# An eight-stage network on one core: loading the second MoE's weights from within the layers' plan, and testing and storing the result by quarters in the last MoE's plan

## The chip, the cores and the metric

The kernel runs on one core of one Trainium2 chip. The core has five engines that run their own streams of instructions: PE (TensorE: matrix products, with a separate path for loading weights), DVE (VectorE), ACT (ScalarE), POOL (GpSimd) and SP (SyncE, which here only issues DMAs). The metric is device time in microseconds (us) of one execution. Three executions of the kernel before gave 1543.07, 1545.97 and 1550.25 us, so the median is 1545.97 us.

## The reference

The activations `x` are 16 sequences of 64 tokens of width 128, so 1024 rows of 128 floats. Eight parts are applied one after the other, each to the layer norm of `x`, and its result is added:

```python
x = x + L0_xcond(ln(x))   # recurrent decoder with attention
x = x + L0_ffn(ln(x))     # m0: mixture of 8 experts and a shared one
x = x + L1_xcond(ln(x))   # perceiver attention
x = x + L1_ffn(ln(x))     # ffn with fake-quantized activations and weights
x = x + L2_xcond(ln(x))   # six decoder layers: self attention, cross attention, ffn
x = x + L2_ffn(ln(x))     # m2: mixture of 8 experts, relu
x = x + L3_xcond(ln(x))   # block
x = x + L3_ffn(ln(x))     # m3: mixture of 8 experts, gelu
```

The quantized ffn scales its activations by the largest absolute value of the whole tensor, which needs a reduction over all partitions. Each of the last two mixtures (MoE) computes, for all 8 experts `e` with 512 hidden units,

```python
h = act(einsum('td,edh->teh', xt, W1) + b1)
y = einsum('teh,ehd->ted', h, W2) + b2
out = einsum('ted,te->td', y, gate)      # gate: softmax over the two largest logits, 0 elsewhere
```

## The kernel before

The eight stages (STAGES, L2870) run in order. `x` is a tile of 128 partitions by 8 groups of 128, held on chip from stage to stage. The stages are computed by halves of 4 groups, and norms and MoE results by quarters of 2 groups (256 rows).

**The planner.** Within a stage no instruction is issued directly. The stage describes operations with `plan.op(engine, ns, emit, deps, ...)`: the engine, an assumed length, the function that emits the instructions, and what it depends on. `_Plan.order` (from L1205 on) is a list scheduler: of the operations that can start, it takes the one that can start first, and at equal times the one with the best rank. A rank is the assumed length of the chain behind the operation, shifted by one digit per operation; the digits of every stage stand as long strings in the table `FIRST` (L1143). `_Plan.fills` then walks through the planned order and puts matmuls of ones in bfloat16 ("units", their result is not used) where the plan sees PE idle, by the plan's own lengths. `_Plan.run` emits everything in that order. So each engine's order is fixed before the program runs, and an operation added to a plan, or another digit, can move the work of every engine. The plan that is named "layers" holds the quantized ffn (`quant_groups`, L2290) and the six layers (`layers`, L2492). Each MoE has a plan of its own, "m2" and "m3", with the same digits for both.

**The start of the layers' plan.** `layers` makes one or two tiles `V` for each kind of attention and half on POOL (`fresh`, L2531 and L2533: a memset and two products with the key mask). `quant_groups` computes the quantized ffn: POOL does a `partition_all_reduce` (L2300) for each scale, DVE turns it into a factor, and PE multiplies the quantized activations (the rows of PE with `guT`). POOL's program holds an instruction without operands ahead of each all-reduce, and another ahead of the next ordinary operation.

**The loads.** `layer_loads` (L2562) puts five loads on SP for each layer (`l_a`, `l_s`, `l_q`, `l_k`, `l_f`), as operations of the plan that take a buffer. The MoE's weights are loaded by `moe` itself (L1830 on): `self.load(name, "moe", parts=8)` issues eight DMAs of 515 KB through L252, and one more for the second bias `bd`. These are outside any plan. What the tile is written over is free long before, and the framework places these DMAs on SP directly behind the first loads of the layers. `begin_later` (L1453) and `load_later` (L1469) are helpers that make a list of such DMAs, `self.later`, which a stage may issue itself one by one; `load` then finds the tile in `self.loaded`.

**The MoE.** For each half and expert, PE makes four products into hidden units (`pj`), ACT applies the activation into `H`, PE makes four down products (`y`, one for each group of 128 rows, L299), and DVE multiplies by the gate and adds to the result, by two groups at a time (`weigh`, L1942). `last` holds the last of these operations for both quarters of a half.

**The end.** After the last stage `_program` stores the whole result with one DMA (L2907) and calls `out_of_range` (L1422). DVE tests that the smallest and largest values kept in `extremes` (eight places each) lie within limits and that every element of `x` times 0 is 0, reduces the answers to one number for each partition, PE sums them over the partitions, and DVE writes `bad`. All engines read `bad` into a register (L2909), and a branch runs a slower, general version of the network if it is set (L2911 on). With the given inputs it is not set.

Of the kernel before, what the change touches and what calls it, by code (L numbers as in the profile page):

```python
# [227 lines left out]
class _Net:  # L228
# [872 lines left out]
    def block(self):  # L1101
# [41 lines left out]
FIRST = {  # L1143
    "perceiver": (
# [7 lines left out]
        "QNpMlVRLXM7eM7sqNaLrqeZwy+9462XsVtwXV3+oFIdXRCfyldrnjzOOJXFybdRMXRbyHYDDfezc/8u48//8/9esm+/1/sQhKu12",  # L1152
        "RENN/o/25/k/w84yusrx21dnimrag7pkzZysdY44s/ivyxYAMAULBPWADAAAAAIAEARAPDBIq1+5xSn29gvqwet9xv7KDDMhXpr0",
        "0yJ09f//n1OjhmFmTKKvNkNGP4lKGWXRwejIpMLdEIWJCWIXJGASMAZEBEPdExZwt3mxz+m+TayIpDKfrMz5/2/+/y7k/Xy++/7/",
        "/0ixxynYfZVYJHSmWCiHJHEAFUAfAqat6us2ev+85gv67hsxyziy8zGcjd89ai2FoSK9Vys1g99vp990f9n8OmUO0KsCKNT8Ms66",
        "fyS90lp1h//0+cTbaVjQQTQlPNPNQTaUBOCKIJLNHKBAJWj5NXR2x16u4u5p83/5//8/t49b5M/2wLpyzlyLWiWH3XhF1LeAJZmn",
        "QIMEO69oqy22nS4k3zwHuOpUljtoH/MDX/cp93jv/cmqdp1cYbw0oVgYLCGTHSPHGvtdyHKEHbTRSNfspjJWHs1Nf2qWjyqYqLjA",
        "CtTl690eqkTeYmusNP3UO6orP5ZB6KxNtBDCsV3AtTWt4UcINFONyVQ3akAsmIFeLdNLGYGC6KqQeren7Sik5qpuXb2I+xAu5eJ6",
        "IJKJMNOKcDEFJLPRMHALJEiBn34wrvuw2zJR0JiNYJfAAArqujcMPAAjmbYoiJleJwlnXROGrXBIGH0RujmS1oTO9p833HZWqs2v",
        "gQEm9+f7y/xybDrDxpZ8//0rTztOqm0kjw0t/87ke5/w/knu806fMCQExPAI9aliAAjWfJ4ItyZ7sd/N0W956724p99//Z//bt3d",  # L1160
        "+b03dIytfWjiDwcmqzkj0ijy33fc7I35XJprvwutr5b1hZmTERqctPahogdw35tj5+lQy+vJISa43Wcm//kWYzpvekUSMAQaQ1wM",
        "LvCkHaMCwC3hxk509236r7Y/94x99x/8/6Yq3lh995WrZj6IOWjYhQIGRSiCRLxNDASRYUVPAKTcHjXDAMAAIABKAM3UamjDXYXs",
        "lpZ753rh5z21260vwt867z748p10xzw13x0afwbAUoLQNfHjbGAAARQiASABAAOAAAJAAwZZq/u+3gVgTcdXqfSXZPQoNSiDTMED",
        "ScGRG/DhSVRLlOHMQDAnKpBDC5z1s327yw06qm6nUvm52ot0ptAJARAAGNEKgnkSjAbPbAggYbcANRGjZwYv1iz2qe/5z/ut9r95",
        "y3Yo6SKKgKDISMWAInlv22YrEliF1dMNLUDCKVurCZBnjAADAKDMKfRldTiYVz2+7732/6/////1xs99p761rlti2tupcjJautf7",
        "75++/8k/9/54kWiZpt6lQzULSWIcIAAslkEZgB2pCnqnfvlJgWILkfUVYNIQXLiJJYFKWXBpJSotct2HTEiGPuh6JBBBoNbdbXZw",
        "8/6/92v9do+UR28OX/i8/49l/55t33+VEhhyNgsbJDDZ3TfrH3iy2iflnhw/5+rkm89vm/18cy/k5567757kU7iR9scqrb38PwvZ",
        "QKRMBKNHdGKJGOTXRMJ1fwZjuyPVPKRd+f86Be6jpoNd4RPammOvo9aCZXWYnbbniXXOMdTtjsNPk6zi/w+9//0b3eDIANHABYUU",
        "ONPGEBFNBFNBBes0Ur1IwheZiMcGISJXVg9o5p8usx0xonSQmjdXcu3731617vunDrA9DvAAaCAAAGAAFTFRlFI6dOULgANmWM1o",
        "YFkppfeKXJ4xMzLbSUU8SDXJEGPTqMELEDDHEFGAFHIAAAEAADFMAjUAADhAAHGUTAzPS3Kv7t9ttwPPVNa3Zlwy8P5VGYqndR7p",  # L1170
        "r/IUVgXNhZwP/1u/krEvdpgbb5MPktW1K1+ZyIulKem9r03ZmuERT8JhHi08/9+ry/8yDQLcMRPXAIZCfotJ9A0uw9t8sm7+Va43",
        "Xd0clbhs/t//v/yrd1h1O1dzsVAk00474yz6r",
# [17 lines left out]
        "yetsvsh+3udKYhQDAIAEZUhLWVMSKtddsHgjlVASDSAJmmXPACAXFYYun3ijZTmd4gViNyLOTbc/uo5/hA8mONRAdIjdjYn8s2i5",  # L1190
        "45555z6z62wzv6Y1aTeUyA4q54x4X2/09++m+uzXty2+kdM1EupHvGtxv66rPwa3T25yk4str677gIyoewvjq2236o/nWQFxWrbx",
        "ssw4/PVbVGBqYDfnU/ew95szgwlLWvbMoPUlpXJfVotaqReq8eTmoiJHDMMHHdym/640//ymz/v0nsb6TkPxnbmey6/nQhS0dW6k",
    ),
    "m3": (
# [155 lines left out]
class _Fast(_Net):  # L1350
# [18 lines left out]
    def load_rest(self, first):  # L1369
# [30 lines left out]
        nc.gpsimd.memset(self.extremes, 1.0)  # L1400
        self.units = self.const.tile([128, 512], BF16, tag="units", name="units")
# [19 lines left out]

    def out_of_range(self):  # L1422

        nc, tc = self.nc, self.tc
        with tc.tile_pool(name="check", bufs=1) as pool, tc.tile_pool(name="check_ps", bufs=1, space=PSUM) as ps:
            z = self.tile(pool, [128, NT, D], "z")
            nc.vector.tensor_scalar(z, self.x, 0.0, None, ALU.mult)
            nc.vector.tensor_scalar(z, z, 0.0, None, ALU.is_equal)
            m = self.tile(pool, [128, 2], "m")
            nc.vector.tensor_reduce(m[:, 0:1], z, AX.XY, ALU.min)  # L1430
            a = self.tile(pool, [128, 2, 8], "a")
            nc.vector.tensor_scalar(a[:, 0, :], self.extremes[:, 0, :], self.HIGH, None, ALU.is_lt)
            nc.vector.tensor_scalar(a[:, 1, :], self.extremes[:, 1, :], self.LOW, None, ALU.is_gt)
            nc.vector.tensor_reduce(m[:, 1:2], a, AX.XY, ALU.min)
            g = self.tile(pool, [128, 1], "g")
            nc.vector.tensor_reduce(g, m, AX.X, ALU.min)
            one = self.tile(pool, [128, 1], "one")
            nc.gpsimd.memset(one, 1.0)
            t = self.tile(ps, [1, 1], "t")
            self.mm(t, g, one)  # L1440
            bad = self.small.tile([1, 1], I32, tag="bad", name="bad", bufs=1)
            nc.vector.tensor_scalar(bad, t, 127.5, None, ALU.is_lt)
        return bad
# [386 lines left out]
    def moe(self, name, act, gated=False, shared=False):  # L1830
# [7 lines left out]
        with ExitStack() as st:  # L1838
# [62 lines left out]
            for h in range(2):  # L1901
# [52 lines left out]
                if shared:  # L1954
                    wide = [128, 4, D]
                    row = lambda n: w(n).unsqueeze(1).to_broadcast(wide)
                    base = plan.op("POOL", 1060, lambda _, h=h: nc.gpsimd.tensor_tensor(
                        half(x, h), half(x0, h), row("ln_b"), ALU.add), ends[2 * h:2 * h + 2])
                    for k in range(2):
                        n = self.quarter_norm(acc, k, last[k])  # L1960
                        two = lambda a, k=k: a[:, 2 * k:2 * k + 2, :]
                        g = plan.op("DVE", 420, lambda t: nc.vector.tensor_tensor(t, t, two(row("ln_g")), ALU.mult),
                                    n, on=n[0])
                        plan.op("DVE", 420, lambda _, h=h, n=n, two=two: nc.vector.tensor_tensor(
                            two(half(x, h)), two(half(x, h)), n[0].slot[1], ALU.add), [g, base])
            with tc.manual_schedule(engines=None):
                plan.run(name, fill=self.fill, banks=("pj", "y"))
# [524 lines left out]
    def layers(self):  # L2492
# [3 lines left out]
        with ExitStack() as st:  # L2496
# [22 lines left out]
            for k, n in (("s", 1), ("c", 2)):  # L2519
# [6 lines left out]
                for h in range(2):  # L2526
# [11 lines left out]
                    plan.buffers(f"V{k}{h}", vs, True)  # L2538
            ctxT = self.ctxT
# [6 lines left out]
            for n in range(NL):  # L2546
# [8 lines left out]
                for h in range(2):  # L2555
                    tops[h] = self.ffn_half(w, h, xs[h], ada, tops[h], x0 if n == NL - 1 else None)
            with tc.manual_schedule(engines=None):
                plan.run("layers", fill=self.fill, banks=("pj", "S", "O"))
# [327 lines left out]
def _program(tc, ins, at, out, stages=range(8)):  # L2886
# [4 lines left out]
    with ExitStack() as ctx:  # L2891
        net = _Fast(ctx, tc, ins, at)
        run = lambda ks: [STAGES[k](net) for k in ks if k in stages]
# [13 lines left out]
        nc.sync.dma_start(out=rows, in_=net.x)  # L2907
# [30 lines left out]
```

## Time and profile before

| what | value |
|---|---|
| median of three runs | 1545.97 us (1543.07 to 1550.25) |
| the profiled execution | 1545.75 us, its span 1543.9 us |
| PE busy | 1387.6 us, 90% of the span |
| DVE, ACT, POOL busy | 751.5, 539.3, 197.7 us |
| chain of waits | PE 81%, DVE 10%, ACT 4%, issue 3% |
| mean granted PE clock | 0.92 of full |
| layers' plan, from the first V tile to the start of m2 | 477 to 1068 us |
| m2, block, m3 | 1068 to 1190, to 1412, to 1534 us |

The span is what the profiler's records of the one core cover; the 1.85 us between it and the execution's time lie outside them. The stages show in the page's table of 40 slices of 38.6 us each, in tenths of the slice for the engines' busy time and for the granted PE clock:

```profile
PE   8666699989996799998999998898999999999997
...
PEclk8555589999998899999999999989999999999999
DMA  2000050000005000001000000003001100000000
```

A digit is read by its place. The 13th slice, from 463 to 502 us, is the end of the perceiver and the start of the layers' plan: the DMA engines are half busy there, and PE is at 6 tenths, the lowest since the first slices. The row of SP in the timeline that belongs to m3's weights shows what one such load is like at another place:

```profile
1189.52 3.97 SPq L252 DMA_DIRECT2D m_sb<-in_m  x8
```

### The profile page before, as it was taken

To read this page: it belongs to the slowest core of one execution; us is meant where nothing else is said; L and a number is where in the kernel's file an instruction comes from. 1 tells how busy PE (TensorE), PEld (TensorE's weight loads), DVE (VectorE), ACT (ScalarE), POOL (GpSimd) and SP (SyncE) were. 2 spreads that over 40 slices of the span, in tenths; PEclk is the share of its full clock that TensorE was granted. 3 is DMA by queue.
4 is the path that set the end of the run, shared out by engine and by line. 5 is a ranking of instruction groups with operands and counts; after the bars stand their busy time and mean duration, and the time that the engine had idled before them with its cause. 6 is when DMAs were issued, how large, how long until landed. Compare 5 with 4: busy or idle time off the path is not lost.

```text
span 1543.9 us, 51104 instructions
## 1 busy us (share of the span) xinstructions
PE 1387.6 (90%) x23238; PEld 986.0 (64%) x23238; DVE 751.5 (49%) x2397; ACT 539.3 (35%) x893; POOL 197.7 (13%) x268
## 2 busy tenths in 40 slices
PE   8666699989996799998999998898999999999997
PEld 5555567757775366565666566565776677775775
DVE  5335441256343875776666576654212544445212
ACT  1111154524330244343434434343333433324342
POOL 1000020020002322222222222211000100001000
PEclk8555589999998899999999999989999999999999
DMA  2000050000005000001000000003001100000000
GB/s 79 5 4 4 4 186 1 0 1 3 3 3 188 17 8 17 28 18 32 18 14 21 7 17 18 17 3 127 26 1 58 54 3 3 3 3 0 1 1 17
DMA packets 14748, 39.16 MB, mean 25 GB/s; under 512 B 2039, under 2 KB 5495, under 8 KB 14522
## 3 DMA queue, kind: packets, MB, share of 16 engines
q1 hardware_dynamic: 13946, 35.19, 6.7%
q8 instruction: 184, 3.01, 0.8%
q10 hardware_dynamic: 576, 0.61, 0.1%
q14 instruction: 42, 0.34, 0.1%
HBM read 35.27 MB, written 0.52 MB: 23 GB/s over the span
## 4 chain that ended last, share of the span: by engine, by line
PE 81%; DVE 10%; ACT 4%; issue 3%; POOL 1%; DMA 0%; ACTq 0%; DVEq 0%; POOLq 0%
PE pj L299 40%; PE y L299 12%; PE O L299 10%; PE S L299 7%; PE cb L299 4%; PE lg L299 2%; PE hh L299 2%; PE pj L2136 1%; PE su L299 1%; PE pj L2663 1%; ACT P L2854 1%; DVE u L2722 1%; DVE nq L2610 1%; DVE co L1768 1%; PE pj L2827 1%
## 5 line engine op out<-in xcount | busy, mean ns | idle before, releaser
L299 PEld LDWEIGHTS y<-m_sb,H 128*128 128x128 f32 x1568 | 186.7, 192 | 35.9 <-issue 31.1
L299 PE MATMUL y<-m_sb,H 128*128 128x128 f32 x1568 | 188.3, 275 | 0.0
L299 PE MATMUL pj<-xT,m_sb 128*128 128x512 f32 x392 | 182.4, 594 | 1.0 <-DVE xT L1875 1.0
L2616 POOL TENSOR_TENSOR nq<-nq,minus_half 128x2 f32<-128x2 f32 x124 | 88.1, 712 | 539.5 <-DVE nq L2613 517.2
L2808 ACT ACTIVATE P<-S 128x1024 f32<-128x1024 f32 x96 | 98.3, 1024 | 133.5 <-PE S L299 133.1
L1918 ACT ACTIVATE H<-pj,m_sb 128x512 f32<-128x512 f32 x128 | 87.9, 687 | 123.7 <-PE pj L299 123.1
L1942 DVE SCALAR_TENSOR_TENSOR x<-y,cw,x 128x128 f32<-128x128 f32 x128 | 36.6, 345 | 151.3 <-PE y L299 151.0
L299 PEld LDWEIGHTS pj<-xT,m_sb 128*128 128x128 f32 x392 | 68.5, 191 | 57.7 <-issue 55.7
L2646 ACT ACTIVATE xn<-x,nq 128x128 f32<-128x128 f32 x104 | 49.7, 489 | 134.0 <-DVE nq L2619 123.5
L2722 DVE TENSOR_TENSOR u<-pj,consts_sb 128x512 f32<-128x512 f32 x96 | 65.6, 688 | 39.7 <-PE pj L299 39.2
L299 PE MATMUL cb<-bd,E 128*32 128x4 f32 x4096 | 65.4, 193 | 0.3
L1918 ACT ACTIVATE H<-pj,b1g,m_sb 128x512 f32<-128x512 f32 x64 | 49.4, 777 | 46.6 <-PE pj L299 43.9
L299 PE MATMUL pj<-xT,l_f 128*128 128x512 f32 x96 | 52.6, 659 | 13.6 <-ACT P L2854 4.2
L299 PE MATMUL pj<-xT,w_sb 128*128 128x512 f32 x128 | 62.9, 603 | 1.9 <-DVE xT L2691 1.9
L299 PEld LDWEIGHTS cb<-bd,E 128*32 128x32 f32 x4096 | 62.5, 153 | 0.8 <-issue 0.6
L2048 DVE COPY QKV<-pj 128x512 f32<-128x512 f32 x56 | 38.7, 690 | 47.2 <-PE pj L299 46.3
L2048 ACT COPY QKV<-pj 128x512 f32<-128x512 f32 x56 | 32.8, 585 | 73.7 <-PE pj L299 73.6
L299 PEld LDWEIGHTS O<-Vc,P 128*64 128x64 f32 x1536 | 49.5, 140 | 13.0 <-issue 8.4
L1775 ACT ACTIVATE H<-hh 128x16 f32<-128x16 f32 x64 | 12.6, 197 | 125.9 <-PE hh L299 125.9
L299 PEld LDWEIGHTS O<-Vs,P 128*64 128x64 f32 x1536 | 48.1, 138 | 11.5 <-issue 8.6
L299 PEld LDWEIGHTS O<-QKV,P 64*32 64x32 f32 (+1 forms) x3072 | 46.1, 107 | 13.9 <-issue 8.1
L299 PE MATMUL O<-Vc,P 128*64 128x18 f32 x1536 | 54.1, 214 | 0.8 <-ACT P L2808 0.6
(358 smaller groups left out, 2475.2 us busy)
## 6 DMA issues: line engine op xcount, KB each, us to landing
w_sb<-in_w SPq DMA_DIRECT2D x7, 681.5 KB, 9.3
m_sb<-in_m SPq DMA_DIRECT2D x8, 515.0 KB, 7.8
m_sb<-in_m SPq DMA_DIRECT2D x8, 514.5 KB, 6.8
m_sb<-in_m SPq DMA_DIRECT2D x16, 256.0 KB, 5.3
l_f<-in_l SPq DMA_DIRECT2D x6, 578.5 KB, 3.7
l_a<-in_l SPq DMA_DIRECT2D x6, 387.0 KB, 3.6
l_s<-in_l SPq DMA_DIRECT2D x6, 384.0 KB, 3.1
w_sb<-in_w SPq DMA_DIRECT2D x4, 512.5 KB, 8.3
```

Source lines behind the costliest of these rows:

```text
L299: self.nc.tensor.matmul(out, lhsT=lhsT, rhs=rhs, start=start, stop=stop, **kw)
L1768: nc.vector.tensor_tensor_scan(co.rearrange("p b k -> p (b k)"), cb[:, :2 * B], XC[:, t, :, :].rearrange("p b k -> p (b k)"), 0.0, ALU.mul ...
L1918: nc.scalar.activation(a[:, c, :], ups[c].slot[1], act, bias=b, scale=g)
L1942: nc.vector.scalar_tensor_tensor(acc[:, k, :], src, g, x0[:, i, :] if first else acc[:, k, :], ALU.mult, ALU.add)
L2048: e(o, i.rearrange("p (b t) -> p b t", t=T) if len(o.shape) == 3 else i)
L2136: t = plan.op("PE", 700, lambda t, On=On: [nc.tensor.transpose(t[:, i * 128:(i + 1) * 128], On.slot[1][:, i * 128:(i + 1) * 128], self.ide ...
L2610: nc.vector.bn_stats(out=t[:, i, 0:6], in_=xk[:, i, :])
L2616: return lambda t: nc.gpsimd.tensor_tensor(t[:, :, b], t[:, :, a], self.minus_half[:, 0:2], ALU.pow)
L2646: nc.scalar.activation(o, xk[:, i, :], AF.Identity, bias=f[1], scale=f[0])
L2663: self.nc.tensor.transpose(t[:, at:at + 128], n[0].slot[1][:, i, :], self.ident)
L2722: us.append(plan.op("DVE", 690, lambda u, t=t, k=k, table=table: nc.vector.tensor_tensor(view(u[:, k, :]), view(t.slot[1]), self.c(table). ...
L2808: P = plan.op("ACT", 1030, lambda P, S=S: nc.scalar.activation(P.rearrange("p (g c) -> p g c", g=4), S.slot[1][:, :, 0:256], AF.Exp, scale ...
```

## The change

There are five parts.

1. A result's quarter is stored and tested as soon as it is done. The new method `settle` adds to m3's plan, for each quarter, a DMA of 256 rows on SP and a test on DVE, and with the first quarter the two tests of the extremes. The answers go to a new tile `fine`. The final store is gone, and `out_of_range` only reduces `fine`, sums over the partitions and writes `bad`. The test of an element, its product with 0 and the comparison, is now one instruction in place of two.
2. m2's nine loads are issued from the layers' plan. `load_later` makes them, and after the ffn of each layer but the first up to three of them are added to the plan on SP, behind that layer's last operations in the plan's reckoning. A load that is issued this way has no wait of its own: nothing was in its tile.
3. The plan "layers" has new digits, for its changed number of operations.
4. The plan "m3" has digits of its own; "m2" keeps the old ones.
5. The tile of ones for the last sum is made at the program's start.

```diff
 FIRST = {
+    "m3": (
...
     "layers": (
-        "QNpMlVRLXM7eM7sqNaLrqeZwy+9462XsVtwXV3+oFIdXRCfyldrnjzOOJXFybdRMXRbyHYDDfezc/8u48//8/9esm+/1/sQhKu12",
...
+        "MDLCe4Wd0zNF0wzCAEMHPEnFRhJEFCdeYkokUOKLbwOaq+3/v9/xh9Kb/8nmHZk2oy+H/ku2/4u474/w2//pva92aKKchggPUOY7",
...
+        self.fine = self.const.tile([128, 20], F32, tag="fine", name="fine")
+        self.one = self.const.tile([128, 1], F32, tag="one", name="one")
+        nc.gpsimd.memset(self.one, 1.0)
...
+    def settle(self, k, x, dep):
+
+        nc, plan = self.nc, self.plan
+        plan.op("SP", 600, lambda _: nc.sync.dma_start(out=self.rows[:, 2 * k:2 * k + 2, :], in_=x), [dep])
+
+        def finite(z):
+            nc.vector.tensor_scalar(z, x, 0.0, 0.0, ALU.mult, ALU.is_equal)
+            nc.vector.tensor_reduce(self.fine[:, k:k + 1], z, AX.XY, ALU.min)
+
+        plan.op("DVE", 650, finite, [dep], "xn")
+        if k:
+            return
+
+
+        def within(_):
+            nc.vector.tensor_scalar(self.fine[:, 4:12], self.extremes[:, 0, :], self.HIGH, None, ALU.is_lt)
+            nc.vector.tensor_scalar(self.fine[:, 12:20], self.extremes[:, 1, :], self.LOW, None, ALU.is_gt)
+
+        plan.op("DVE", 350, within)
+
     def out_of_range(self):
...
-            z = self.tile(pool, [128, NT, D], "z")
-            nc.vector.tensor_scalar(z, self.x, 0.0, None, ALU.mult)
-            nc.vector.tensor_scalar(z, z, 0.0, None, ALU.is_equal)
...
-            nc.vector.tensor_reduce(g, m, AX.X, ALU.min)
-            one = self.tile(pool, [128, 1], "one")
-            nc.gpsimd.memset(one, 1.0)
-            t = self.tile(ps, [1, 1], "t")
-            self.mm(t, g, one)
+            g, t = self.tile(pool, [128, 1], "g"), self.tile(ps, [1, 1], "t")
+            nc.vector.tensor_reduce(g, self.fine, AX.X, ALU.min)
+            self.mm(t, g, self.one)
...
+                if name == "m3":
+                    for j in range(2):
+                        self.settle(2 * h + j, half(x, h)[:, 2 * j:2 * j + 2, :], last[j])
...
+            self.later = []
+            self.load_later("m2", "moe", 8)
+            self.load_later("m2_bd", "moe_b2")
...
                 for h in range(2):
                     tops[h] = self.ffn_half(w, h, xs[h], ada, tops[h], x0 if n == NL - 1 else None)
+                for _ in range(3 if n else 0):
+                    if self.later:
+                        plan.op("SP", 1500, lambda _, begin=self.later.pop(0): begin(None), tops)
...
+        net.rows = rows
...
-        nc.sync.dma_start(out=rows, in_=net.x)
         bad = net.out_of_range()
```

## The prediction

> **What bounds the kernel now.** I read the page first: the chain that ended last is TensorE (PE) for 81% of the span, VectorE (DVE) 10%, ScalarE 4%, "issue" 3%, and PE is busy 1387.6 of 1543.9 us. So only what shortens PE's work or its waits counts. The change touches three places, which I read in order of time: the start of the layers' plan, the six layers, and the end with the last MoE.
>
> The start, in the timeline of all engines (start, length, engine, line, operation, count; in brackets the idle time before and what ended it):
>
> ```profile
> 487.36 4.21 SPq L252 DMA_DIRECT2D m_sb<-in_m  x8
> 487.57 0.56 POOL L2533 TENSOR_TENSOR Vc<-consts_sb,m8c 128x64 f32<-128x64 f32 x2
> 498.57 0.38 POOL L2300 PARTITION_ALL_REDUCE qs<-qs  x1 [10.44 <-issue]
> 501.52 1.86 PE L299 MATMUL S<-oT,guT 128*128 128x512 bf16 x4 [12.50 <-ACT oT L2336]
> 507.06 0.56 POOL L2533 TENSOR_TENSOR Vc<-consts_sb,m8c 128x64 f32<-128x64 f32 x2 [7.11 <-issue]
> ```
>
> and a little later in the same view:
>
> ```profile
> 516.32 0.38 POOL L2300 PARTITION_ALL_REDUCE qs<-qs  x1 [5.86 <-DVE u L2722]
> 523.49 2.73 POOL L2725 TENSOR_TENSOR krc<-u 128x512 f32<-128x512 f32 x2 [6.79 <-DVE u L2722]
> ```
>
> PE idles 12.5 us because the quantized ffn's scale needs an all-reduce over partitions on GpSimd (POOL). POOL is free at 488.1 and starts it at 498.57, with nothing that the profile shows to wait for. Each time POOL goes from ordinary operations to the all-reduce or back, it stands still: 10.44, 7.11, at most 5.86, at most 6.79 us. The first two lie under the 4 MB load of the second MoE's weights (m2), issued from 487.36 on.
>
> The busy times by stretch (from:to, length, then busy us and count of PE, weight load, DVE, ScalarE, POOL; PE clock granted, DMA share, GB/s): the six layers, two stretches under the m2 load, one under the third MoE's load.
>
> ```profile
> 540.00:629.00 89.00, 81.06 (x1344) 53.79 (x1343) 59.34 (x184) 36.06 (x54) 20.60 (x22) 0.94 0.04 12
> 629.00:718.00 89.00, 80.19 (x1421) 55.06 (x1420) 61.05 (x183) 34.70 (x50) 21.41 (x22) 0.98 0.08 22
> 718.00:808.00 90.00, 82.05 (x1343) 54.37 (x1342) 61.72 (x189) 35.53 (x51) 22.53 (x23) 1.00 0.08 22
> 808.00:890.00 82.00, 76.10 (x1326) 52.05 (x1325) 50.76 (x168) 33.88 (x49) 19.01 (x21) 0.98 0.06 17
> 890.00:976.00 86.00, 76.34 (x1361) 52.53 (x1361) 56.68 (x179) 34.74 (x50) 20.02 (x21) 1.00 0.06 16
> 976.00:1067.00 91.00, 78.62 (x1278) 52.53 (x1278) 50.91 (x156) 34.41 (x48) 19.40 (x20) 0.91 0.03 9
> 489.00:495.00 6.00, 0.03 (x1) 0.00 (x0) 0.00 (x0) 0.00 (x0) 0.00 (x0) 0.75 1.01 354
> 495.00:501.00 6.00, 0.00 (x0) 0.00 (x0) 1.88 (x6) 0.25 (x1) 1.38 (x2) 0.50 1.03 398
> 1192.00:1201.00 9.00, 7.95 (x27) 3.53 (x27) 7.98 (x42) 1.37 (x3) 4.50 (x7) 0.83 1.02 412
> ```
>
> A layer takes 82 to 91 us for the same work: the planned order decides it, not an engine's capacity. The DMA engines are full from 489 to 501, and move 354 GB/s where the same kind of load alone moves 412.
>
> The end, in the timeline of PE and then of DVE:
>
> ```profile
> 1527.90 5.52 PE L299 MATMUL y<-m_sb,H 128*128 128x128 f32 x48
> ```
>
> ```profile
> 1533.46 1.12 DVE L1942 SCALAR_TENSOR_TENSOR x<-y,cw,x 128x128 f32<-128x128 f32 x4 [2.45 <-PE y L299]
> 1534.65 0.68 DVE L1427 TENSOR_SCALAR z<-x 128x1024 f32<-128x1024 f32 x1
> 1535.36 0.69 DVE L1428 TENSOR_SCALAR z<-z 128x1024 f32<-128x1024 f32 x1
> 1536.09 1.22 DVE L1430 TENSOR_REDUCE m<-z 128x1 f32<-128x1024 f32 x1
> 1537.88 0.15 DVE L1442 TENSOR_SCALAR bad<-t 1x1 int32<-1x1 f32 x1 [0.37 <-PE t L299]
> ```
>
> PE's last down product ends at 1533.42; then 4.6 us of tests by DVE alone until `bad` is there at 1538.03. The 5.9 us from there to the span's end are the register load, the branch and its instruction fetch, which the edit leaves alone.
>
> **The change, part by part. 1. m2's load leaves the start.** It goes from the queue of SP at 487 to behind the second, third and fourth layers' ffn, three pieces each. What hid it before: PE was idle there anyway. Gain: if the code switch of POOL at 488 costs what the later ones do (5.86 at most in the one that saw no load, 7.11 in one that saw the load's end) instead of 10.44, it is 3.3 to 4.6 us shorter. Loss: in the new order POOL makes one more fresh V tile before the first all-reduce, 1.06 + 0.56 = 1.62 us (rows of L2531 and L2533), so it is free at 489.7. Net of the first switch −1.7 to −3.0 us. The second switch (7.11) can lose at most 7.11 − 5.86 = 1.3 more, and PE already has other work then. The ends are −4.4 and, if the 10.44 is the first switch's own price, +1.6. I take −3.0: the first switch at its unburdened row, nothing for the second.
>
> A rule of the Trainium skill has to be weighed here (GPSIMD Engine Reference, 2.1 Instruction dispatch): the first call to a freshly loaded GpSimd kernel pays an instruction load of about 6 us that no profile row shows. The unburdened rows agree (5.86, 6.79); by the rule the 10.44 has 4.4 us of something else in it. A second rule speaks against the gain (DMA: Bandwidth & Descriptors, Queues, rings and completion order): each DMA engine goes round the queues packet by packet, so a burst on one queue should hold up a code fetch on another by about a packet at a time, far less than 4 us. By that rule part 1 would be a loss of 1.6 us; by the rows a gain of 3.0. I go with the rows: engines at a share of 1.01 while 354 instead of 412 GB/s move say that something is squeezed in that stretch.
>
> **2. The three groups on SP.** Each `begin` issues one 515 KB DMA with no wait of its own. Its price on SP is 4.21/8 = 0.53 us, so a group holds SP 1.6 us and moves 1.5 MB, about 4 us at 400 GB/s. Behind it stand the next layer's loads, which run a whole layer (over 80 us) ahead of use; DMA share in these stretches is 0.06 to 0.08. The m2 stage begins at 1068, the last group lands near 815. Cost 0; if a layer load did stand behind a group and was wanted at once, 4 us each, 12 in all. In the layers POOL makes no all-reduce, so no code switch lies under the groups.
>
> **3. The layers' new order.** All engines' instructions are re-ordered in the whole plan, while the counts of work stay equal. The only difference in count is fill: bf16 matmuls that the planner puts where it sees PE idle. In layers 1 to 5 there are 59 instead of 76, in layer 0 and before it 69 instead of 68. A row gives their price, 5.12/23 = 0.22 us:
>
> ```profile
> 477.43 5.12 PE L299 MATMUL pj<-units 128*128 128x512 bf16 x23 [0.35 <-ACT sdrow L2271]
> ```
>
> 17 × 0.22 = 3.7 us of planned idle less. The plan's idle is not the chip's: PE is idle in the six layers 527 less 474 us, 53 us in all. The ends: all layers as the best, 82 us, or as the slow ones, 90 (6 × 82 = 492 and 6 × 90 = 540 against 527): −35 and +13. Between ends so far apart I take the planned idle, −3.6.
>
> **4. m3's order and the tests by quarters.** The stage is PE at 120.94 of 122 us; nothing inside can gain. Two y tiles get their third product's successor directly behind a weighing of the same tile, so PE waits for DVE there: about 0.7 us each (a weighing of two rows takes 0.61, and the PE waits behind one show 0.67), +1.4. The tests of the first three quarters run on DVE, busy 29.89 of 122 us in this stage: hidden. The extremes tests go too. At the end remain: weighing of the last quarter 0.61 (half of the 1.12 row), the fused test on 128 × 256 about 0.25, its reduce 0.37 (a 128 × 256 reduce elsewhere), the last reduce 0.16, PE's sum with its latency 0.5, bad 0.15 and some latency: 2.2 instead of 4.6, −2.4. The four stores of 128 KB go out while PE works; the final store of before also ended (1537.5) ahead of `bad`, so it was hidden already. Nothing waits behind SP's waits for a quarter: no load is left to issue in that stage. Net −1.0; ends −2.4 (no waits) and +0.5.
>
> **The sum.** −3.0 + 0 − 3.6 − 1.0 = −7.6 us, made against the profiled run: its span 1543.9 goes to 1536.3, with the 1.85 us outside it 1538.15. The profiled run (1545.75) is 0.2 below the median, which changes nothing. **1538 us.**
>
> **The rivals.** What can be told from no change is 0.5%, 7.7 us: faster means below 1538.2, slower above 1553.7.
> - B, the new order gains more than its fills: two of the four slow layers (89 to 91) come near the best (82), −12 instead of −3.6, total near 1530. For it: 53 us of PE idle in the layers; against it: the planner's count shows only 17 fills less.
> - C, the 10.44 us are the first switch's own price (the second rule): +1.6 − 3.6 − 1.0 = −3.0, 1542.8.
> - D, the other side: the layers' new order puts each layer on the pace of the slowest. DVE is 59 to 62 us of 89 in the slow layers and 51 of 82 in the fast one, and with all engines re-ordered a DVE operation ahead of the one PE wants costs each layer. Six layers at 90 are +13, with −4.0 from the rest 1554.8; it decides from +4 us on, where it outweighs all the rest, and makes the kernel measurably slower from +12. For it: the same code already takes 82 and 91; against it: fewer planned idles.
> - E, the change doesn't do what it says, for instance because the m2 load is still hoisted: the order built shows SP issuing it in three groups, so small; 1545.
>
> **How the numbers follow.** A (forecast, own range 1533 to 1544) 0.40, B 0.28, C 0.13, D 0.14, E 0.05. The forecast sits on the edge of what counts as faster: of A 0.24 is faster and 0.16 the same; B is faster; C, E and 0.02 of D are the same; 0.12 of D is slower. Together 0.52, 0.36, 0.12. The range, 1527 to 1550, holds A, C, E, most of B and D's lower part.
>
> **What would show it.** m2's DMAs in threes near 630, 720 and 810; POOL's idle before its first all-reduce 6 to 7 us and PE's wait before the S product near 9.5; layers 1 to 5 together shorter by some 4 us; two waits of 0.7 us for a weighing in m3; 2.2 us from PE's last y to `bad`. Wrong if the idle stays above 10 us (then C), or if any layer's stretch leaves its old length by over 5 us, which would make the layers' order the whole story.

## The result and the profile after

The changed kernel takes 1534.23 us (median of 20 runs, 1526.21 to 1545.83), the kernel before 1546.06 us (20 runs). The ratio is 0.9932, with a 95% interval from 0.9912 to 0.9952: 10.5 us faster (7.4 to 13.6). The forecast was 1538 (−7.6).

The page of the profiled execution (1530.63 us) begins with the span and the busy time of PE:

```profile
span 1528.8 us, 51048 instructions
...
PE 1373.4 (90%) x23191; PEld 980.1 (64%) x23222; DVE 759.6 (50%) x2401; ACT 540.1 (35%) x893; POOL 197.2 (13%) x268
```

PE is busy 14 us less than before, in a span that is 15 us shorter, though the products are the same and only 16 fills are gone. That is no measure of the new order: PE's busy time goes with the clock that the run was granted. The run of e1_load_moved below, with all the fills and nearly the order of before, has PE busy for 1373.9 us at a mean clock of 0.927; the run of before had 1387.6 us at 0.920. First the three places in the order of the prediction. The start, from the timeline of all engines (start, length, engine, line, operation; in brackets the idle time before and its releaser):

```profile
491.13 0.56 POOL L2548 TENSOR_TENSOR Vc<-consts_sb,m8c 128x64 f32<-128x64 f32 x2
497.30 0.38 POOL L2315 PARTITION_ALL_REDUCE qs<-qs  x1 [5.60 <-issue]
498.76 2.08 PE L299 MATMUL pj<-ctxT_sb,l_k 128*128 128x512 f32 x2 [5.71 <-DVE u L2744]
500.64 0.63 PE L299 MATMUL S<-oT,guT 128*128 128x512 bf16 x1
505.47 0.56 POOL L2548 TENSOR_TENSOR Vc<-consts_sb,m8c 128x64 f32<-128x64 f32 x2 [6.79 <-issue]
```

POOL's idle before the first all-reduce is 5.60 us instead of 10.44. That it is a change of POOL's code can be seen in the packed trace, which holds instructions that the timeline leaves out: at the beginning of this idle time stand two instructions MODIFY_POOL_CONFIG (at 488.07 before, at 491.64 now), two more at that of the way back (499.90 and 498.63), and no other work of POOL until its end. From the first V tile to the S product it is 21.43 us (479.21 to 500.64) instead of 24.24 (477.28 to 501.52): −2.8 us, where −3.0 was forecast. PE's idle time before S, 12.50 us in one piece before, now has 5.71 us as its longest piece (9.5 was forecast), since the new order puts two key products in front of S. The m2 load, in the timeline of SP, goes out in three groups, at the ends of layers 1, 2 and 3 (the prediction gave the times of the ends of layers 0, 1 and 2):

```profile
706.64 1.61 SPq L1477 DMA_DIRECT2D m_sb<-in_m  x3
...
793.81 1.60 SPq L1477 DMA_DIRECT2D m_sb<-in_m  x3
...
893.12 0.82 SPq L1477 DMA_DIRECT2D m_sb<-in_m  x2
```

At the end, the last quarter's weighing, its test and the two last steps remain on DVE:

```profile
1520.47 1.16 DVE L1954 SCALAR_TENSOR_TENSOR x<-y,cw,x 128x128 f32<-128x128 f32 x4
1521.66 0.29 DVE L1432 TENSOR_SCALAR xn<-x 128x256 f32<-128x256 f32 x1
1521.99 0.42 DVE L1433 TENSOR_REDUCE fine<-xn 128x1 f32<-128x256 f32 x1
1522.50 0.17 DVE L1451 TENSOR_REDUCE g<-fine 128x1 f32<-128x20 f32 x1
1523.04 0.15 DVE L1454 TENSOR_SCALAR bad<-t 1x1 int32<-1x1 f32 x1 [0.37 <-PE t L299]
```

PE's last y product ends at 1520.98, `bad` is there at 1523.19: 2.2 us. The view of PE's waits in this stage shows the price, two waits for a weighing:

```profile
PE y L299 <- DVE x L1954: 1.4, 2, 0.7
```

(us in total, how many, the longest.) The layers, in the view of busy times by stretch: start of the plan, then layers 0 to 5, cut at each layer's last product with `l_f` (from:to, length, then busy us and count of PE, weight load, DVE, ScalarE, POOL; PE clock granted, DMA share, GB/s):

```profile
479.21:500.64 21.43, 13.77 (x108) 7.47 (x110) 13.05 (x51) 2.68 (x6) 11.83 (x21) 0.93 0.40 130
500.64:621.10 120.46, 102.24 (x1442) 63.93 (x1449) 90.09 (x272) 46.73 (x71) 30.43 (x35) 0.94 0.05 13
621.10:706.10 85.00, 78.37 (x1412) 55.71 (x1413) 61.10 (x178) 35.24 (x50) 20.41 (x21) 0.98 0.08 23
706.10:793.30 87.20, 75.06 (x1294) 50.92 (x1297) 56.11 (x177) 34.36 (x50) 21.37 (x22) 1.00 0.13 40
793.30:892.10 98.80, 89.16 (x1467) 58.69 (x1469) 68.16 (x200) 38.18 (x53) 24.77 (x25) 0.97 0.09 30
892.10:968.40 76.30, 68.96 (x1250) 48.87 (x1252) 48.52 (x162) 31.75 (x47) 16.37 (x18) 1.00 0.12 35
968.40:1051.90 83.50, 70.43 (x1271) 48.17 (x1274) 53.65 (x156) 34.31 (x48) 19.74 (x20) 1.00 0.03 9
```

Cut in the same way, the kernel before has 24.2, 127.5, 89.3, 90.1, 82.0, 85.7 and 91.2 us, together 590.0 against 572.7. So all that the two traces differ by lies here: 2.8 us at the start, 14.5 in the layers. A stretch ends at a product and doesn't hold the same work in both kernels: layer 3 has 1469 weight loads on PE in the changed kernel and 1326 in e1, whose order is nearly that of before. But the last layer's clock is 1.00 here and 0.91 before. One trace of each can't say whether the order or the clock did that. The runs can: each of them has its span and its mean granted clock. In the trace the clock has two values in the main: of 566 stretches of 1 us in the layers of before, 510 have 1.0 and 36 have 0.5. Below, "span × clock" is the product of both, the time with the stretches at half clock counted half.

| kernel | runs | median us | mean clock | mean of span × clock |
|---|---|---|---|---|
| before (beside the first eight experiments) | 87 | 1545.6 | 0.9231 | 1424.7 |
| e1_load_moved | 22 | 1541.5 | 0.9244 | 1423.3 |
| e2_load_early | 15 | 1538.4 | 0.9227 | 1417.7 |
| changed | 20 | 1534.2 | 0.9250 | 1417.9 |
| e3_end_only | 14 | 1546.3 | 0.9234 | 1426.2 |
| e4_after_more_fills | 6 | 1537.5 | 0.9285 | 1425.4 |
| e6_new_then_old | 22 | 1542.4 | 0.9263 | 1428.3 |
| e7_old_then_new | 22 | 1546.6 | 0.9218 | 1424.2 |
| e8_pool_first | 6 | 1529.0 | 0.9275 | 1417.6 |
| e9_old_no_fills | 6 | 1560.4 | 0.8980 | 1400.3 |
| e10_new_no_fills | 22 | 1559.3 | 0.8952 | 1395.1 |
| e11_pool_first_again | 6 | 1529.3 | 0.9272 | 1417.0 |
| e12_after_again | 6 | 1534.2 | 0.9247 | 1417.0 |

The standard error of the last column is between 0.2 and 1.0. The table has all runs, also the eight slowest of e10_new_no_fills, which the ratio of its fast runs (1.0046) leaves out. The experiments ran on three chips; the last column of before is 1425.2, 1424.2 and 1425.1 on them, so their rows can be compared within about 1 us.

The product has a limit. If it were a constant of a kernel, 0.01 of clock would go with 16.7 us of span. Among the runs of one kernel it goes with 7 to 15 us, so the product rises with the clock. A wait at half clock, too, counts only half in it, whether or not a higher clock would have shortened it. Where a reading rests on it, the difference at equal clock (with 11.6 us for 0.01, the slope within the kernels with fills and 14 or more runs, taken together) is given beside it. This is an estimate from the runs' own figures.

### The profile page after: what moved, and what is told of

Same layout as the page of the kernel before. It is cut to its first block, busy times and chain, and to the rows that moved or that the text cites. A ratio compares the mean times of both kernels' runs of the same rounds, so it can differ in the third digit from the quotient of the medians.

```text
span 1528.8 us, 51048 instructions
## 1 busy us (share of the span) xinstructions
PE 1373.4 (90%) x23191; PEld 980.1 (64%) x23222; DVE 759.6 (50%) x2401; ACT 540.1 (35%) x893; POOL 197.2 (13%) x268
## 4 chain that ended last, share of the span: by engine, by line
PE 81%; DVE 10%; ACT 4%; issue 3%; POOL 1%; ACTq 0%; DVEq 0%; POOLq 0%
PE pj L299 40%; PE y L299 12%; PE O L299 9%; PE S L299 7%; PE cb L299 4%; PE lg L299 2%; PE hh L299 2%; PE su L299 2%; PE pj L2151 2%; DVE u L2744 1%; PE pj L2685 1%; DVE qx L2798 1%; ACT P L2830 1%; DVE nq L2632 1%; DVE co L1780 1%
## 5 line engine op out<-in xcount | busy, mean ns | idle before, releaser
L299 PE MATMUL pj<-xT,l_s 128*128 128x512 f32 x96 | 49.8, 624 | 6.0 <-DVE x L2499 3.0
```

What stands on the lines that cost most here:

```text
L299: self.nc.tensor.matmul(out, lhsT=lhsT, rhs=rhs, start=start, stop=stop, **kw)
```

## The experiments

**e1_load_moved: the load alone.** Before, with m2's loads in the layers' plan; the loads get no digit of the table, so that every other operation keeps its own.

```diff
+            self.later = []
+            self.load_later("m2", "moe", 8)
+            self.load_later("m2_bd", "moe_b2")
...
+                for _ in range(3 if n else 0):
+                    if self.later:
+                        plan.op("SP", 1500, lambda _, begin=self.later.pop(0): begin(None), tops)
...
+        if name == "layers":
+            given = iter(digits)
+            digits = "".join("g" if o.engine == "SP" and o.takes is None else next(given) for o in self.ops)
```

The order on PE, ScalarE and POOL is that of before; on DVE one pair of neighbours is exchanged.

> The kernel before with nothing changed but m2's nine loads, which go into the layers' plan in three groups; the digits, the fills and the last MoE stay as before. Theory (the burst of m2's load lengthens the code switch of POOL, the rest of the gain is the layers' order): POOL's idle before its first all-reduce falls from 10.4 to 5.6-6.2 us, PE's wait before the S product from 12.5 to about 8 us, time 1541 to 1543 (ratio 0.997), the layers' stretches behind 540 us unchanged. Rival 1 (a first switch costs about 10 us by itself): idle 10 to 11 us, time as before. Rival 2 (moving the load is the whole gain of the change): time near 1534, ratio 0.993.

Measured: ratio 0.9977 (0.9965 to 0.9989), −3.6 us. From its POOL timeline:

```profile
495.76 0.38 POOL L2303 PARTITION_ALL_REDUCE qs<-qs  x1 [5.74 <-issue]
```

and its busy times by stretch, cut as above:

```profile
479.16:498.71 19.55, 10.85 (x49) 5.56 (x51) 10.96 (x48) 2.68 (x6) 10.28 (x18) 0.87 0.42 142
...
626.70:715.90 89.20, 79.87 (x1419) 55.42 (x1422) 61.08 (x183) 34.58 (x50) 21.43 (x22) 0.98 0.08 22
715.90:807.50 91.60, 83.14 (x1343) 55.17 (x1346) 61.72 (x188) 35.55 (x51) 22.92 (x24) 0.98 0.12 39
807.50:888.00 80.50, 74.24 (x1322) 51.20 (x1326) 50.67 (x167) 33.91 (x49) 18.62 (x20) 1.00 0.11 37
888.00:973.70 85.70, 75.58 (x1352) 52.23 (x1357) 56.87 (x179) 34.75 (x50) 20.05 (x21) 1.00 0.10 31
973.70:1059.50 85.80, 72.27 (x1272) 48.95 (x1276) 50.94 (x156) 34.32 (x48) 19.45 (x20) 0.98 0.03 9
```

The start is 4.7 us shorter (19.55 instead of 24.24), and 1.9 us shorter than the changed kernel's 21.43, since the old order has one V tile less ahead of the all-reduce. Layers 1 to 4, under which the three groups land, take 347.0 us against 347.1: the groups cost nothing. The last row is a warning: 85.8 us with a clock of 0.98, where the same order took 91.2 in the trace of before with 0.91. The clock of a stretch differs from run to run of one and the same order.

**e2_load_early: everything but the load.** The changed kernel, with `moe` loading m2 as before and operations that do nothing in place of the groups.

```diff
-            self.later = []
-            self.load_later("m2", "moe", 8)
-            self.load_later("m2_bd", "moe_b2")
...
-                for _ in range(3 if n else 0):
-                    if self.later:
-                        plan.op("SP", 1500, lambda _, begin=self.later.pop(0): begin(None), tops)
+                for _ in range(3 if 0 < n < 4 else 0):
+                    plan.op("SP", 1500, lambda _: None, tops)
```

> The changed kernel with m2's nine loads issued again at the start of the layers' plan as before; digits, fills and the last MoE as in the changed kernel. Theory: POOL's idle before its first all-reduce rises from 5.6 to about 10 us, and the time by 3 to 5 us over the changed kernel, to 1537-1539 (ratio to before 0.9955). Rival 1: idle stays near 5.6 and time at 1534, so the burst is not what lengthened the switch. Rival 2 (the load is the whole gain): 1546, ratio 1.000.

Measured: ratio 0.9952 (0.9938 to 0.9965), 1538.4 us, 0.2% (3.1 us) over the changed kernel's ratio. POOL:

```profile
501.08 0.38 POOL L2315 PARTITION_ALL_REDUCE qs<-qs  x1 [9.10 <-issue]
```

and a stretch of its busy times, POOL being free from 491.98 on (the last but one number is the DMA share):

```profile
492.00:501.00 9.00, 2.28 (x35) 1.31 (x34) 0.98 (x2) 0.00 (x0) 0.00 (x0) 0.81 0.71 276
```

The S product comes 24.91 us after the first V tile, 3.5 us later than in the changed kernel. The burst is not quite that of before: the timeline of SP has six of the eight pieces at 487.56 and the last two only at 505.03, behind the switch. So the DMA engines are full for some 6.3 us of it (0.71 of the 9 us). Both ways of looking at the load give 3 to 4 us (this second one, from the intervals of the two ratios, with an uncertainty as large as itself, 3.7 us), and leave 7 for the rest: e2 stands 7.4 us below before (5.4 to 9.6) with the load at the start. Its mean clock is that of before (0.9227 and 0.9231), its span × clock 7.0 lower, its span at equal clock 7.4. So the rest is not a luckier clock.

**e3_end_only: the end alone.** The changed kernel with the layers' plan of before.

```diff
+    "m3": (
...
-        nc.sync.dma_start(out=rows, in_=net.x)
...
+                if name == "m3":
+                    for j in range(2):
+                        self.settle(2 * h + j, half(x, h)[:, 2 * j:2 * j + 2, :], last[j])
```

> The kernel before with only the end changed: tests and stores by quarters and the new digits of m3; the load of m2 and the layers' plan as before. Theory: two waits of 0.7 us of PE for a weighing in m3, 2.2 us from PE's last y product to bad instead of 4.6, time -1.0 us (1545, ratio 0.9994). Rivals: -2.4 us (the waits cost nothing), 0 (the waits eat it all); only the trace can tell these apart, the times scatter by more.

Measured: ratio 1.0003 (0.9987 to 1.0018). From its view of PE's waits:

```profile
PE t L299 <- DVE g L1451: 1.8, 1, 1.8
PE y L299 <- DVE x L1954: 1.4, 2, 0.7
```

and from that of before:

```profile
PE t L299 <- DVE g L1436: 4.2, 1, 4.2
```

Both steps are there: PE's wait for the last test is 1.8 us instead of 4.2, and two waits of 0.7 are new. From the issue of m3's load to `bad` it is 348.00 us (1193.89 to 1541.89) against 348.51 before: a gain of 0.5 in the trace, and nothing that the times can show.

**e4_after_more_fills.** The changed kernel with 84 more fills in the layers.

```diff
+        if name == "layers":
+            self.LEVEL = 0.52
         fills = self.fills(best, banks) if fill else {}
```

> The changed kernel with more bf16 fills in the layers' plan (the planner's level of PE activity 0.52 instead of 0.42: 84 more matmuls of ones, 0.22 us each, 18 us if none lay in a gap); all orders are the same. Theory that the layers' gain is PE's granted clock (fewer stretches at half clock behind stalls): the half-clock time left in the layers, 6.7 us in the changed kernel's trace, nearly goes, the runs scatter less (within 6 us instead of 20), and the time is 1534 to 1542, the fills costing more than the clock brings. Rival (the clock in the layers doesn't matter, only the order): scatter stays, time rises by the fills outside gaps, 8 to 18 us, to 1542-1552.

Measured: 1537.5 us (1534.02 to 1539.07), ratio 0.9945 (0.9923 to 0.9966). In the table, the 84 fills raise span × clock by 7.5 us (6.3 at equal clock), so less than 0.1 us each and not 0.22, and the higher clock gives 5 us of that back. So a higher clock is to be had (0.9285), but it isn't what the layers' gain consists of: e2 has that gain without it. The scatter falls as the first theory said, from 20 us in 20 runs to 5 in 6, though few runs say little about that.

**e5_half_burst: a dose.** The changed kernel with four of m2's pieces at the start, five loads in the groups.

```diff
+            self.early, self.later[:4] = self.later[:4], [lambda _: None] * 4
...
+        if name == "m2":
+            for begin in self.early:
+                begin(None)
```

> The changed kernel with four of m2's eight pieces (2 MB instead of 4.4 MB) issued at the start of the layers' plan, the other five loads in the groups as in the changed kernel. Theory (while the DMA engines are full POOL's switch goes on at 5.6/9.1 = 0.6 of its pace, at full pace afterwards): the half burst ends 2 to 3 us after POOL has begun its first switch, so the idle before the first all-reduce is 6.3 to 7.0 us. Rival 1 (any load under way when the switch begins costs its whole delay): 9 us. Rival 2 (only the end of the whole load matters, POOL waits for it): the idle ends with the burst's last packet, below 5.6 us there, so 5.6.

Measured, POOL's timeline first, and then the busy times by stretch after POOL became free at 488.3:

```profile
495.58 0.38 POOL L2318 PARTITION_ALL_REDUCE qs<-qs  x1 [7.24 <-issue]
```

```profile
488.00:490.00 2.00, 1.73 (x12) 0.53 (x12) 1.34 (x2) 0.00 (x0) 0.34 (x2) 1.00 0.98 354
490.00:491.00 1.00, 0.92 (x32) 0.78 (x28) 0.00 (x0) 0.00 (x0) 0.00 (x0) 1.00 0.98 396
491.00:492.00 1.00, 0.00 (x0) 0.00 (x0) 0.00 (x0) 0.00 (x0) 0.00 (x0) 1.00 0.96 383
492.00:493.00 1.00, 0.00 (x0) 0.00 (x0) 0.00 (x0) 0.00 (x0) 0.00 (x0) 1.00 0.28 99
```

The DMA engines are full for 3.9 us of the switch (1.7 + 1.0 + 1.0 + 0.3), and it takes 7.24 us: more than the forecast 6.3 to 7.0, since the burst reached 1 us further into it. At 0.6 of the pace during those 3.9 us and the full pace afterwards, a switch of 5.6 us would take 5.6 + 0.4 × 3.9 = 7.2. A little load costs a little, a large one much: 5.6 without, 7.24 with 3.9 us of full engines (four pieces), 9.10 with some 6.3 us (e2's six), and 10.44 with the engines full all along (eight). Both rivals fall. The pace itself is only rough: from 5.6 us of switch it comes out as 0.58, 0.45 and 0.54 in the three. The 0.6 of the expectation took e2's engines for full during all of its 9.1 us.

**e6_new_then_old and e7_old_then_new: which layers.** The new digits for one half of the layers' plan, the old ones for the other, with the cut ahead of layer 3.

```diff
+        if name == "layers":
+            given, cut = iter("".join(FIRST["old"])), self.starts[3]
+            old = ["g" if o.engine == "SP" and o.takes is None else next(given) for o in self.ops]
+            digits = [d if k < cut else e for k, (d, e) in enumerate(zip(digits, old))]
```

(`k >= cut` in the second.)

> The changed kernel with the new digits for the quantized ffn and layers 0 to 2, and the digits of before for layers 3 to 5; all else as in the changed kernel. Theory (the order's gain comes in layers 0 to 2: idle plus busy time reckoned at full clock fell there by 4.3 + 4.2 + 2.9 us, and rose by 3.7 in layers 3 to 5): 1530 to 1534, ratio 0.990 to 0.992, if the old digits still fit the state that they meet. Rival (the order acts as a whole, and digits out of their setting are as good as none): 1540 or more. Rival (the gain is the 17 fills): as the changed kernel plus the fills that come back, 1535 to 1537.

> The changed kernel with the digits of before for the quantized ffn and layers 0 to 2 and the new digits for layers 3 to 5; all else as in the changed kernel. Theory: the gain of layers 0 to 2 is lost, 1542 to 1547 (ratio about 1.000, the load's gain of 3.5 kept). Rival (digits out of their setting): 1550 and more. Rival (the gain lies in the last layers): 1534 to 1537.

Measured: ratios 0.9997 (0.9982 to 1.0013) and 1.0012 (0.9997 to 1.0027), though both keep the load's 3.6 us. My theory, that the gain sits in layers 0 to 2, falls. In e6's trace layers 0 to 2 are nearly as quick as in the changed kernel (318.6 us from the first V tile to layer 2's last product, there 314.1, in e1 328.3), but layer 3 with its old digits takes 93.9 us, where the same digits take 80.5 in e1. The new order leaves work of one layer for the next one to do (the weight loads of layer 3, above), and a stretch from one product to the next doesn't show that. e7 took the time that was expected of it, but so would any order that has lost the gain. What fits both is the first rival, that the order acts as a whole. Which of its exchanges brings the gain stays open.

**e8_pool_first, and e11_pool_first_again beside e12_after_again: less work on POOL ahead of the first switch.** The changed kernel with two things moved on POOL at the start.

```diff
                     def fresh(V, h=h, m8=m8, k=k):
-                        nc.gpsimd.memset(V, 0.0)
+                        if V is not self.fresh["c", 1, "first"]:
+                            nc.gpsimd.memset(V, 0.0)
+                        if (k, h) == ("s", 0):
+                            nc.gpsimd.memset(self.fresh["c", 1, "first"], 0.0)
...
+        if name == "layers":
+            i, = [i for i, b in enumerate(best) if b[2] is self.late]
+            j = [j for j, b in enumerate(best) if j > i and b[2].engine == "POOL"][15]
+            best.insert(j, best.pop(i))
```

> The changed kernel with two things moved on POOL at the start of the layers' plan, the same work otherwise: the clearing of one V tile goes into POOL's 1.6 us wait for the key mask, and the making of another V tile (1.6 us, first used near 544) goes from ahead of the first all-reduce to where POOL is idle near 532. Theory (POOL's work ahead of its first code switch sets when the quantized ffn starts): POOL is free 2.6 us earlier, the first all-reduce and PE's S product come 2.4 to 2.7 us earlier after the first V tile, time 1531 to 1532, ratio to before 0.991. Rival (the chain through the norms and DVE's maxima is as late as POOL): less than 1 us. Rival (the second all-reduce or a later wait gives it back): the S product is earlier, the time is not.

> e8_pool_first again, beside the changed kernel on the same chip. Theory: 2 to 3 us faster than e12_after_again. Rival: the difference seen between the first runs was their scatter, within 1 us.

> The changed kernel as it is, on the chip of e11_pool_first_again: 1532 to 1537, ratio to before 0.991 to 0.995.

Measured: 1529.0 us (ratio 0.9907, 0.9881 to 0.9934), again 1529.3 (0.9906, 0.9886 to 0.9927) beside 1534.2 of the changed kernel (0.9933, 0.9907 to 0.9959). The 12 runs together are some 5 us below the changed kernel's median, and by the differences of the ratios 3.9 and 4.2 us, more than the 2 to 3 that were expected. Each interval overlaps with the changed kernel's own; the means of the 12 runs and of the changed kernel's 26 differ by 4.5 us, with an uncertainty of 2.8. POOL's timeline of e8:

```profile
475.27 1.06 POOL L2552 MEMSET Vs<- 128x1152 f32 x1 [119.66 <-PE pj L299]
476.26 1.08 POOL L2554 MEMSET Vc<- 128x1152 f32 x1
...
491.26 0.38 POOL L2319 PARTITION_ALL_REDUCE qs<-qs  x1 [5.76 <-issue]
```

The all-reduce starts 16.0 us after the first V tile's begin instead of 18.1 (497.30 − 479.21), and the S product 19.3 instead of 21.4: 2.1 us of the gain. The rest doesn't show in span × clock (1417.6 and 1417.0, as the changed kernel's 1417.9 and 1417.0) but in the mean clock, 0.927 to 0.9275 against 0.925. In the trace PE's longest idle time before S is 2.79 us now, where it was 5.71; that this is what spares a stretch at half clock fits, but was not tried apart.

**e9_old_no_fills and e10_new_no_fills: the order without fills.** e1 and the changed kernel, no fills in the layers.

```diff
-        fills = self.fills(best, banks) if fill else {}
+        fills = self.fills(best, banks) if fill and name != "layers" else {}
```

> The kernel before with m2's load in groups (as in e1_load_moved) and without any bf16 fills in the layers' plan (144 matmuls of ones less), to be read against e10_new_no_fills. Theory (the fills are nearly free, since 84 more of them cost 3.3 us in all, and the gain is the order): 7 us slower than e10_new_no_fills, as with fills (1541.5 to 1534.2), or 6 to 8; its clock is lower than with fills, time 1540 to 1555. Rival (half of the gain is the 17 fills less, 3.7 us): only 3 to 4 us slower than e10_new_no_fills.

> The changed kernel without any bf16 fills in the layers' plan (128 matmuls of ones less). Theory: 6 to 8 us faster than e9_old_no_fills; lower clock than the changed kernel's 0.925, time 1534 to 1548. Rival (half of the gain is the fills): 3 to 4 us faster than e9_old_no_fills.

Measured: 1560.4 and 1559.3 us. Both expectations fail in the times: the difference is 1.1 us, and with runs that go from 1541.65 to 1577.68 in e10 it is uncertain by some 6 us. In span × clock the new order is 5.2 us shorter (1395.1 instead of 1400.3, standard error 1.0), without a single fill in either; with fills, e1 against the changed kernel, it is 5.4 (0.6). At equal clock it is 4.5 us without fills (with 12.9 us for 0.01, the slope of e10's own runs) and 6.1 with them. So most of the gain is there without any fills, in this reckoning, though not in elapsed time. A share of the fills, such as the 1.4 us that 16 of them would cost at e4's price, isn't excluded, and neither are the 3 to 4 us of the rival. e10's mean clock is lower than e9's (0.8952 and 0.8980), which their scatter doesn't resolve. The fills pay for themselves many times over in both: 144 of them take e1 from 1560.4 to 1541.5.

## Why the prediction came out as it did

**The start: right.** −3.0 was forecast and −2.8 is in the traces, from the two terms of the forecast: the switch is 4.84 us shorter (4.6 forecast), and the extra V tile takes back 1.9 between e1 and the changed kernel (1.62 forecast). In the times, moving the load alone gives −3.6 (−1.7 to −5.4), and taking it out of the changed kernel 3.1. (The far end of this term's range is −4.2 by its own numbers, 1.62 − 4.58 − 1.25, and not −4.4.) The choice between the two rules and the row was decided by e1, e2 and e5: the switch takes 5.5 to 5.8 us without a load beside it, which agrees with the 6 us that the Trainium skill gives for the first call to freshly loaded GpSimd code (GPSIMD Engine Reference, 2.1 Instruction dispatch), and up to 10.4 with full DMA engines, which the round of the DMA engines through their queues (DMA: Bandwidth & Descriptors, Queues, rings and completion order) gave no reason to expect. By which path the code comes, and where it is held up, no record here shows.

**The three groups: right**, at 0; e1's layers 1 to 4 are 347.0 and 347.1 us.

**The layers' order: the sign was right, the size half, and the term wrong.** The step said "17 × 0.22 = 3.7 us of planned idle less", and took it as the whole. Measured from e1 to the changed kernel it is 0.45%, 7 us, and from before to e2 7.4, both with the end, which adds nothing that can be seen. The term of the sum that failed is the price of a fill as a measure of the order: added fills cost less than 0.1 us each (e4), so the 16 are worth 1.4 us and not 3.6, and with none at all the new order keeps 4.5 us at equal clock, or 5.2 in span × clock (e9, e10). What gives most of the gain is the sequence of the real work on all engines. Whether a slightly higher clock has a share in it isn't resolved (0.9244 and 0.9250, standard errors 0.0005 and 0.0009). The sign was right, but hardly for the reason given: a count of fills says nothing of how the real work is arranged, and e6 and e7 show that mixing the two sets of digits loses the gain. To that extent the sign was luck. The prediction had a larger gain of the order as rival B, with −12 for the layers at 0.28; the result lies between the forecast and B, and within the forecast's own range.

The prediction's own sign of being wrong here, a layer's stretch more than 5 us off its old length, came in: layer 0 is 7.0 us shorter, layer 3 16.8 longer, layers 4 and 5 are 9.4 and 7.7 shorter. It said that the order would then be the whole story; of the 10.5 us it is about 7. As a sign it was badly chosen, since work moved across the ends of the stretches. Layers 1 to 5 together are 7.5 us shorter (438.3 to 430.8) where 4 were forecast, but 7.7 of that are layer 5, which had the lower clock before.

**The end: the parts right, the sum not resolved.** Two waits of 0.7 and 2.2 us after the last product were forecast, and are in the trace to the tenth. Their sum, −1.0, is −0.5 in e3's trace, since the rest took some tenths more, and +0.5 (−2.0 to 2.8) in its times.

**The rivals.** C fell with e1: the first switch has no price of its own. D (every layer on the slowest's pace) fell too: layer 3 did become longer, 82.0 to 98.8 us, but it holds more of the work, and layer 4 gave 9.4 us of it back. E fell with the three groups in the timeline of SP.

The profiled pair alone would mislead: its layers differ by 14.5 us, of which some 12 are half clock that the one run of before had and the one run after hadn't (PE's busy time times the part of the clock that was missing, summed over stretches of 1 us in the layers: 23.4 us before, 11.7 after). Over all runs the two clocks are 0.9231 and 0.9250.

## What to carry to other kernels

This reordering could not be sized by its fills or by the idle time that the planner saw; give such a term a wide range, as rival B did, and measure it with everything else held fixed. Compare orders by runs, not by one trace each, and look at span and granted clock together: a difference in the clock of one pair of traces may be chance. Ahead of a stretch where one engine has to change its code, look at what the DMA queues carry then, and at what else that engine does first.

## What the runs showed of the hardware

The granted clock differs from run to run of one program: 0.919 to 0.929 over 44 runs of before on one chip, 0.918 to 0.933 over those of the changed kernel, and the time follows it, from 1526.2 us at 0.933 to 1545.8 at 0.918. The changed kernel without fills in the layers (e10) spreads more widely still, from 0.881 to 0.909.

A code switch of POOL with little or no DMA traffic takes 5.5 to 5.8 us on the way to the first all-reduce and 6.7 to 7.5 us on the way back (ten traces without a burst). On the way there it goes on at roughly half its pace while the DMA engines are full (5.6 us of switch in 10.44; 7.24 with 3.9 us of full engines).
